# Where the last layer norm's VectorE work stands inside the next row pair's threshold search

## The chip, the cores and the metric

The kernel runs on one core of one Trainium2 chip. The metric is device time in microseconds (us); the kernel before takes 3777.57 us, the median of three runs (3777.3 to 3778.19). TensorE (PE) multiplies matrices, ScalarE (ACT) evaluates functions and copies, VectorE (DVE) and GpSimd (POOL) do elementwise work, and SyncE (SP) starts DMAs. Every engine works through its own queue in order and waits on semaphores for the others.

## The reference, cut to what matters

There are two graph layers on a matrix of N = 2708 rows and 512 columns. Each layer first takes `h = relu(layernorm(x))`, and its result is added to x. The first layer is a dense graph attention with 8 heads. The second, where the change is, makes two diffusion steps and ends with a layer norm of its own:

```python
for s in range(STEPS):                       # STEPS = 2
    A = _adj_from_feats(Xa, W1, W2, W3)      # nucleus attention, below
    Xf = Rf @ Xf
    Xb = Rb @ Xb
    Xa = A @ Xa
    Z = Z + (Xf @ U1[s] + Xb @ U2[s] + Xa @ U3[s])
Y = X + Z
mu = Y.mean(axis=-1, keepdims=True)
var = Y.var(axis=-1, keepdims=True)
return (Y - mu) / jnp.sqrt(var + LN_EPS) * gamma + beta

def _adj_from_feats(Xa, W1, W2, W3):
    logits = (Xa @ W1) @ W2 @ (Xa @ W3).T
    # per row: sort, cumulative softmax, keep the largest entries up to a mass of 0.9
    ...
    return jax.nn.softmax(masked, axis=1)
```

So in the last step every row needs logits against all 2708 keys, a threshold that keeps 90% of its softmax mass, the product of the kept weights with Xa, the three U products, and then the layer norm over its 512 columns, plus the residual x.

## The kernel before, in words

The rows lie in 22 tiles of 128 (the last has 20 rows). In the second layer they are worked in 11 pairs of tiles (`pairs`), and a loop `for g in range(-1, NP)` (L1158) runs over the pairs as a pipeline written out by hand: the orders on PE, ACT, DVE and SP are those of the program (`manual_schedule`, L1139). Only POOL's order is chosen by the planner of the framework, which goes by program order and by when it reckons an instruction ready.

One turn g of the loop, in the last step (s = 1), has in program order:

- `lg[g + 2].products()` (L509): the logits of pair g + 2. PE multiplies (L517), ACT copies from PSUM to the tiles p (L519, four of them).
- `normed` for the two tiles of pair g - 1, in the list `norms` (L1167). `normed` (L1074) takes the moments of the finished rows y at once: bn_stats and bn_aggr on DVE (L137, L138), then 1/sqrt on POOL (L139, L140). It starts the load of the residual xb on SP (L1079, tiles xw, two buffers shared with the load of L1067) and returns `rest`: two DVE instructions on 512 columns per tile (L1082, L1083) and the DMA of the result from POOL's queue (L1084).
- `search(lg[g + 1], ...)` (L593): DVE finds the threshold of pair g + 1. A head of small instructions brackets it from trial points; then `rounds` (L653) makes four rounds in this step (two in step 0). A round is a row of small instructions that choose a threshold th, one `mass` per tile (L624: all 2708 columns, two inputs, a sum) and small ones that narrow the bracket (L673 to L678). After the first round (`it == 0`) it calls `early()`, after `it == 1`'s threshold it calls what `early` returned.
- `early` (L1176) begins `exp()` of pair g + 2: the row maxima on DVE (L544); ACT's exponentials and their sums, POOL's trial points (`points`, L559 to L572, ending in the negated thresholds nth, L569) and ACT's twelve looks at them (L549) are put in the list `fills`. In the last step it returns a function that runs all `rest` of `norms`.
- `choose` (L692), then `late` (L1181): `attended` of pair g on PE. Its weights `keep` are transposed (L1004), copied by ACT (L1008, `at`) and multiplied with the values (L1023). `fills` and the diffusion products (`others`, L959) are dealt out between its steps. Then `mixed` (L1040) multiplies by U1, U2, U3 (L1051), and ACT (L1064) and POOL (L1068) put together the rows y that the next turn norms.
- `finish` (L793): DVE writes `keep` of pair g + 1 (L800, first of all; two buffers, which are those that PE has read for pair g) and extracts the cut; a switch on a value (L884) runs further instructions where entries are tied (L736 to L752). `rden` (L901) is its last instruction.

In the last turn (g = 10) there is no search: `normed` and `rest` of pair 9 run directly (L1203). After the loop those of pair 10 follow.

Of the kernel before, what the change touches and what calls it, by code (L numbers as in the profile page):

```python
# [53 lines left out]
def kernel(  # L54
# [77 lines left out]
    def moments(pool, src, pr):  # L132

        st = pool.tile([P, 6], F32, name="ln_st")
        mv = pool.tile([P, 2], F32, name="ln_mv")
        rs = pool.tile([P, 1], F32, name="ln_rs")
        nc.vector.bn_stats(st[:pr], src)  # L137
        nc.vector.bn_aggr(mv[:pr], st[:pr])  # L138
        nc.gpsimd.tensor_scalar(rs[:pr], mv[:pr, 1:2], LN_EPS, None, op0=OP.add)  # L139
        nc.gpsimd.tensor_tensor(rs[:pr], rs[:pr], nhalf[:pr], OP.pow)  # L140
        return mv[:pr, 0:1], rs[:pr]
# [346 lines left out]
    class Logits:  # L488
# [33 lines left out]
        def exp(self, looks=True):  # L522
# [68 lines left out]
            return steps  # L591

    def search(lg, looked, early, late):  # L593

        (wide, small, _), grp, ps_, tot, thr, s = lg.pools, lg.grp, lg.p, lg.tot, lg.thr, lg.s
        v = nc.vector
        nx = NEXT[s]
# [18 lines left out]
        def aim(dst, th):  # L618
            v.scalar_tensor_tensor(dst, th, AIM[s], lg.cap, op0=OP.mult, op1=OP.min)
            v.scalar_tensor_tensor(dst, tot, 1.0 - P_NUC + CURVE, dst, op0=OP.mult, op1=OP.add)  # L620
            v.reciprocal(dst, dst)

        def mass(i, pr, th, dst):
            v.scalar_tensor_tensor(junk_b[:pr], ps_[i][:pr], th, ps_[i][:pr],  # L624
                                   op0=OP.is_ge, op1=OP.mult, accum_out=dst)
# [27 lines left out]
        def rounds(n, aim_at=None):  # L653
            for it in range(n):
                v.tensor_tensor(d, ends[:, 1, 0:2], ends[:, 0, 0:2], op=OP.subtract)
                v.tensor_scalar(d[:, 1], d[:, 1], -1e-12, None, op0=OP.min)
                v.reciprocal(fr, d[:, 1])
                v.tensor_mul(fr, fr, ends[:, 0, 1])
                v.tensor_scalar(fr, fr, -0.95, -0.05, op0=OP.max, op1=OP.min)
                v.tensor_mul(fr, fr, d[:, 0])  # L660
                v.tensor_tensor(cur[:, 0], ends[:, 0, 0], fr, op=OP.subtract)
                v.tensor_mul(th, cur[:, 0], cur[:, 0])
                v.tensor_mul(th, th, th)
                if it in (aim_at or ()):
                    v.tensor_copy(fr, g0)
                    aim(g0, th)
                    v.tensor_tensor(fr, fr, g0, op=OP.subtract)
                    v.tensor_tensor(ends[:, :, 1], ends[:, :, 1], fr.unsqueeze(1).to_broadcast([P, 2, G]), op=OP.add)
                if it == 1 and begun:
                    begun.pop()()  # L670
                for i, pr in tiles:
                    mass(i, pr, th[:pr, i:i + 1], cur[:pr, 2, i:i + 1])
                v.tensor_tensor(fr, lg.top, cur[:, 2], op=OP.subtract)  # L673
                v.reciprocal(fr, fr)
                v.tensor_tensor(cur[:, 1], fr, g0, op=OP.subtract)
                v.scalar_tensor_tensor(side, cur[:, 1].unsqueeze(1).to_broadcast([P, 2, G]), 0.0, sides,
                                       op0=OP.is_ge, op1=OP.not_equal)
                v.copy_predicated(ends, side.unsqueeze(2).to_broadcast([P, 2, 3, G]),  # L678
                                  cur.unsqueeze(1).to_broadcast([P, 2, 3, G]))
                if it == 0 and aim_at is not None:  # L680
                    begun.append(early())

        begun = []
        rounds(ROUNDS[s], (0,) if s else ())
# [219 lines left out]
    for s in range(STEPS):  # L904
        last = s == STEPS - 1
        with ExitStack() as st:
# [20 lines left out]
            def values():  # L927
                for t in range(NT):
                    nc.sync.dma_start(out=va[:rows[t], t, :], in_=(xa_d if last else va_d)[cols[t], :])
# [49 lines left out]
            def paced(steps, n):  # L979
                for step in steps[:n]:  # L980
                    step()
                del steps[:n]

            def diffused(grp):
                out_ = []
                for i in range(2):
                    for t in grp:
                        x = work.tile([P, D], F32, name=f"x{i}")
                        nc.sync.dma_start(out=x[:rows[t]], in_=xfb_d[i, cols[t], :])
                        out_.append(x)  # L990
                return out_[:len(grp)], out_[len(grp):]
# [82 lines left out]
            def normed(t, y):  # L1074

                pr = rows[t]
                mean, rs = moments(small, y[:pr], pr)
                xb = work.tile([P, D], F32, name="xw", bufs=2)
                nc.sync.dma_start(out=xb[:pr], in_=xb_d[cols[t], :])  # L1079

                def rest():
                    nc.vector.scalar_tensor_tensor(y[:pr], y[:pr], mean, g_b[:pr], op0=OP.subtract, op1=OP.mult)  # L1082
                    nc.vector.scalar_tensor_tensor(y[:pr], y[:pr], rs, xb[:pr], op0=OP.mult, op1=OP.add)  # L1083
                    nc.gpsimd.dma_start(out=out[cols[t], :], in_=y[:pr])  # L1084

                return rest
# [52 lines left out]
            with tc.manual_schedule(engines={PE, ACT, DVE, SP}):  # L1139
                counted, spread = ranks() if last else (None, None)  # L1140
                lg = [Logits(pools, s, grp, keys, rank) for grp in pairs[:1]]
                lg[0].queries()
                lg[0].products()
                steps = lg[0].exp(looks=False)
                if last:
                    counted()
                for step in steps:
                    step()
                half = []
                lg += [Logits(pools, s, grp, keys, rank) for grp in pairs[1:2]]  # L1150
                lg[1].queries()
                for step in part(half, 0):
                    step()
                values()
                done = []
                ready = None
                looks, left = [], []
                for g in range(-1, NP):  # L1158

                    fills = []  # L1160
                    if g + 2 < NP:
                        lg[g + 2].products()
                    paced(looks, len(looks))
                    if g + 3 < NP:
                        lg.append(Logits(pools, s, pairs[g + 3], keys, rank))
                        lg[g + 3].queries()
                    norms = [normed(t, y) for t, y in done] if last else []  # L1167
                    done = []

                    rows_in = []  # L1170
                    if g >= 0:
                        left.append(lambda g=g: rows_in.extend(diffused(pairs[g])))
                    others = left + part(half, g + 2)
                    left = []

                    def early(g=g):  # L1176
                        if g + 2 < NP:
                            fills.extend(lg[g + 2].exp())
                        return lambda: [rest() for rest in norms]

                    def late(g=g):  # L1181
                        if g >= 0:
                            keep, rden = ready
                            if g:
                                paced(others, 1)
                            xa, v_t = attended(pairs[g], keep, rden, fills, others, lambda: turned_rows(pairs[g], rows_in[0]))
                            done.extend(mixed(pairs[g], v_t, rows_in[1], xa, others, fills))
                            paced(others, len(others))
                            paced(fills, len(fills))
                            return  # L1190


                        if last:
                            spread()
                        paced(fills, 5 + G * NA)
                        paced(others, NT if last else NT - NT // 2)
                        looks.extend(fills)
                        left.extend(others)

                    if g + 1 < NP:  # L1200
                        ready = search(lg[g + 1], g >= 0, early, late)
                    else:
                        for rest in norms:  # L1203
                            rest()
                        late()
                if last:
                    for rest in [normed(t, y) for t, y in done]:
                        rest()
# [31 lines left out]
```

## Time and profile before

| | |
|---|---|
| median of 3 runs | 3777.57 us |
| the profiled execution | 3774.21 us, of which the span from first to last instruction 3772.1 us |
| PE, busy share of the span | 90% |
| DVE | 69% |
| ACT | 41% |
| POOL | 22% |
| DMA | 167 GB/s of HBM traffic over the span |
| mean granted TensorE clock | 0.956 |

The last step runs from about 2430 us to the end of the span. The page shows shares of the whole span, so a single stage has to be read from the timeline: each line there has the start in us from the span's start, the duration in us, engine, line of the kernel, operation, output<-inputs, shapes, and how many equal instructions were merged. In square brackets stand the idle time of the engine just ahead of it and the instruction that ended this idle time. In lists of waits the three numbers are the total in us, how many times, and the longest in us.

### The profile page before, as it was taken

The page shows a single profiled execution, that of the slowest core. Times are in us where ns is not written, and L with a number is a line of the kernel's source. Part 1 is how long each engine was busy: PE and PEld are TensorE (multiplying, and loading weights), DVE is VectorE, ACT ScalarE, POOL GpSimd, SP SyncE. Part 2 cuts the span into 40 slices and gives each one's busy share as a digit, 9 for nine tenths or more (in the row PEclk, how much of TensorE's full clock was granted, in tenths as well). Part 3 has the DMA queues.
Part 4 walks back from the last instruction along what each step waited for, and adds up shares of the span by engine and source line. Part 5 has one row for each costly group of instructions (what it writes and reads, how often), then busy time and mean ns, then how long its engine had stood idle before and what let it go on. Part 6 is the DMA issues. An engine that isn't in the chain of part 4 may idle for free. (4 is left out here: it accounts for less than half of the span.)

```text
span 3772.1 us, 35425 instructions
## 1 busy us (share of the span) xinstructions
PE 3383.3 (90%) x11143; PEld 1760.6 (47%) x11143; DVE 2611.1 (69%) x4814; ACT 1540.1 (41%) x2334; POOL 838.2 (22%) x1187
## 2 busy tenths in 40 slices
PE   8999999999855898989898998668999999999988
PEld 4433333333533455545454453435555665556443
DVE  4588888989946526474554641967779798777992
ACT  2343202111025565546566621335544556445511
POOL 4115151423331121121212020302121211212101
PEclk9999999999977999999999998989999999999989
DMA  3476424233154554454545352845556665567552
GB/s 115 159 255 219 155 78 140 85 99 114 44 167 143 193 197 158 154 184 146 195 146 206 114 176 83 302 130 206 187 202 225 229 209 192 197 212 243 184 192 88
DMA packets 276457, 634.07 MB, mean 168 GB/s; under 512 B 37209, under 2 KB 70441, under 8 KB 273243
## 3 DMA queue, kind: packets, MB, share of 16 engines
q1 hardware_dynamic: 249183, 540.99, 43.3%
q0 software_dynamic: 27024, 90.30, 6.3%
q8 instruction: 89, 1.46, 0.2%
q14 instruction: 161, 1.32, 0.1%
HBM read 509.07 MB, written 122.10 MB: 167 GB/s over the span
## 5 line engine op out<-in xcount | busy, mean ns | idle before, releaser
L1023 PE MATMUL a<-va,at 128*128 128x512 f32 (+2 forms) x1936 | 898.0, 603 | 58.0 <-ACT at L1008 57.9
L959 PE MATMUL q<-hl,s_r 128*128 128x512 f32 x2904 | 821.8, 429 | 67.2 <-DMA s_r<-s_d 65.7
L429 PE MATMUL po<-e,fw 128*65 128x512 f32 (+4 forms) x2112 | 840.4, 553 | 30.0 <-DVE e L427 22.2
L427 DVE SCALAR_TENSOR_TENSOR e<-r_b,kk,a_c 128x512 f32<-128x512 f32 (+4 forms) x1056 | 752.3, 741 | 68.8 <-PE po L429 18.2
L959 PEld LDWEIGHTS q<-hl,s_r 128*128 128x128 f32 x2904 | 545.8, 190 | 312.4 <-issue 147.5
L549 ACT ACTIVATE junk_a<-p,nth 128x2708 uint8<-128x2708 f32 (+1 forms) x240 | 613.0, 2554 | 93.2 <-POOL nth L569 89.6
L429 PEld LDWEIGHTS po<-e,fw 128*65 128x65 f32 (+1 forms) x2112 | 286.5, 140 | 544.2 <-issue 269.1
L1023 PEld LDWEIGHTS a<-va,at 128*128 128x128 f32 (+2 forms) x1936 | 339.6, 188 | 428.2 <-issue 347.2
L1051 PE MATMUL a<-u_k,v_t 128*128 128x512 f32 (+1 forms) x1056 | 490.8, 601 | 20.9 <-ACT xa L1031 15.1
L624 DVE SCALAR_TENSOR_TENSOR junk<-p,th 128x2708 bf16<-128x2708 f32 (+1 forms) x132 | 402.2, 3047 | 4.0
L1008 ACT COPY at<-t 128x512 f32<-128x512 f32 (+3 forms) x308 | 139.8, 476 | 439.4 <-PE t L1004 439.2
L1051 PEld LDWEIGHTS a<-u_k,v_t 128*128 128x128 f32 (+1 forms) x1056 | 188.6, 186 | 239.6 <-issue 187.0
L517 PE MATMUL t<-keys,q_t 128*128 128x452 f32 x528 | 167.9, 444 | 117.0 <-ACT p L519 95.0
L800 DVE SCALAR_TENSOR_TENSOR keep<-p,th 128x2708 f32<-128x2708 f32 (+1 forms) x44 | 133.4, 3033 | 132.4 <-PE t L1004 131.1
L181 DVE TENSOR_SCALAR split_hl<-xe 128x512 int32<-128x512 int32 (+1 forms) x44 | 19.0, 432 | 275.6 <-ACT xe L965 232.6
L802 DVE MAX8 vn<-keep 128x8 f32<-128x2708 f32 (+1 forms) x66 | 196.8, 2981 | 2.3
L519 ACT COPY p<-t 128x452 f32<-128x452 f32 (+2 forms) x264 | 132.7, 539 | 149.8 <-DVEq L884 78.9
L517 PEld LDWEIGHTS t<-keys,q_t 128*128 128x128 f32 x528 | 91.8, 211 | 188.7 <-ACT p L519 149.5
L411 ACT ACTIVATE s_c<-a_c 128x512 fp32r<-128x512 f32 (+3 forms) x132 | 76.2, 577 | 248.3 <-DMA a_c<-in_adj_t_dram 123.2
L1004 PE MATMUL t<-ident,keep 128*128 128x128 f32 (+1 forms) x968 | 146.4, 273 | 21.9 <-DVE keep L752 16.5
L1004 PEld LDWEIGHTS t<-ident,keep 128*128 128x128 f32 (+1 forms) x968 | 114.5, 138 | 105.1 <-issue 76.9
L544 DVE TENSOR_REDUCE nmx<-p 128x1 f32<-128x2708 f32 (+1 forms) x44 | 129.2, 2966 | 40.3 <-ACT p L519 40.1
(294 smaller groups left out, 3105.1 us busy)
## 6 DMA issues: line engine op xcount, KB each, us to landing
s_r<-s_d SPq DMA_DIRECT2D x330, 256.0 KB
hl<-vhl_d SPq DMA_DIRECT2D x132, 512.0 KB
u_k<-in_L_gnn_U_dram SPq DMA_DIRECT2D x264, 256.0 KB
hl<-fhl_d SPq DMA_DIRECT2D x132, 512.0 KB
hl<-bhl_d SPq DMA_DIRECT2D x132, 512.0 KB
arow<-in_adj_dram SPq DMA_DIRECT2D x21, 1354.0 KB
s_d<-s_c SPq DMA_DIRECT2D x88, 256.0 KB
a_c<-in_adj_t_dram SPq DMA_DIRECT2D x84, 256.0 KB
```

The lines of the kernel that those rows point to most:

```text
L427: nc.vector.scalar_tensor_tensor(e[:pr, :cw], r_b[:pr, i, :cw], kk[:pr, t, hd:hd + 1], a_c[t][:pr, :cw], op0=OP.max, op1=OP.mult)
L429: nc.tensor.matmul(po[i][:, :cw], lhsT=fw[:pr, t, hd, :], rhs=e[:pr, :cw], start=(t == 0), stop=(t == NT - 1))
L517: nc.tensor.matmul(pl[:, :c1 - c0], lhsT=q[:, i], rhs=self.keys[:, c0:c1], start=(i == 0), stop=(i == 1))
L549: nc.scalar.activation(junk[:pr], self.p[i][:pr], func, **kw)
L624: v.scalar_tensor_tensor(junk_b[:pr], ps_[i][:pr], th, ps_[i][:pr], op0=OP.is_ge, op1=OP.mult, accum_out=dst)
L800: v.scalar_tensor_tensor(keep[i][:pr], ps_[i][:pr], t, ps_[i][:pr], op0=OP.is_lt, op1=OP.mult, accum_out=left[:pr, i:i + 1] if e else None)
L802: v.max(vs, keep[i][:pr])
L959: nc.tensor.matmul(half[j], lhsT=s_r[:, j * P:(j + 1) * P], rhs=hl[:, h], start=(c == 0 and h == 0), stop=(c == NT - 1 and h == 1))
L1004: nc.tensor.transpose(pt[:rows[c], j, :pr], keep[i][:pr, cols[c]], ident[:pr, :pr])
L1008: nc.scalar.copy(at[:r, j0:j1, :pr], pt[:r, j0:j1, :pr])
L1023: nc.tensor.matmul(pa[:pr], lhsT=at[:rows[c], j, :pr], rhs=va[:rows[c], c, :], start=(c == 0), stop=(c == NT - 1))
L1051: nc.tensor.matmul(pz[i][:rows[t]], lhsT=v_t[i][:, k, :rows[t]], rhs=u_k, start=(n == 0 and k == 0), stop=(n == 2 and k == KD - 1))
```

## The change

`early` returns a list of two functions instead of one function, and `rounds` runs one of them per round, ahead of the masses, from `it == 2` on. The first calls `normed` for both tiles (the moments, the load of xb), the second runs their `rest`. So at the head of the turn nothing of the layer norm is left; its moments stand ahead of the masses of the third round, and its end ahead of those of the fourth, where before they stood ahead of the search and ahead of the masses of the second. `norms` now holds the pairs (t, y) themselves; the last turn makes `normed` of them directly. In step 0 `norms` is empty, as before.

```diff
@@ rounds, in search @@
-                if it == 1 and begun:
-                    begun.pop()()
+                if it > 1 and begun:
+                    begun.pop(0)()
                 for i, pr in tiles:
                     mass(i, pr, th[:pr, i:i + 1], cur[:pr, 2, i:i + 1])
...
                 if it == 0 and aim_at is not None:
-                    begun.append(early())
+                    begun.extend(early())
@@ the loop over the pairs @@
-                    norms = [normed(t, y) for t, y in done] if last else []
+                    norms = done if last else []
                     done = []
...
                     def early(g=g):
                         if g + 2 < NP:
                             fills.extend(lg[g + 2].exp())
-                        return lambda: [rest() for rest in norms]
+                        held = []
+                        return [lambda: held.extend(normed(*x) for x in norms), lambda: [rest() for rest in held]]
...
                     else:
-                        for rest in norms:
+                        for rest in [normed(*x) for x in norms]:
                             rest()
                         late()
```

## The prediction

> **What bounds the kernel now.** I read the page first. TensorE is busy 90% of the span, VectorE 69%; so VectorE time counts only where TensorE stands waiting for it.
>
> ```profile
> span 3772.1 us, 35425 instructions
> PE 3383.3 (90%) x11143; PEld 1760.6 (47%) x11143; DVE 2611.1 (69%) x4814; ACT 1540.1 (41%) x2334; POOL 838.2 (22%) x1187
> ```
>
> Then the waits of the second step (2500 to 3772 us). VectorE loses 159.2 us to the statistics that the change moves, 63.1 of them in one wait at the end of the kernel, which stays. TensorE waits for VectorE once, 16.5 us.
>
> ```profile
> DVE ln_st L137 <- POOL yo L1068: 159.2, 18, 63.1
> PE t L1004 <- DVE keep L752: 16.5, 1, 16.5
> ```
>
> Third, TensorE's timeline. I call "turn g" the stretch that starts with the normed rows of pair g-1, holds the search of pair g+1 on VectorE, and attended and mixed of pair g on TensorE. Turns 1 to 8 follow each other every 116.7 us (their first statistics start at 2660.3, 2776.3, ... 3360.5, 3477.1) with TensorE nearly full (114.0 of 116.6 us in turn 7). Only turn 9 begins late: the search in turn 8 meets a tie and ends at 3597.9, while TensorE was done at 3581.5.
>
> ```profile
> 3526.71 3.70 PE L1023 MATMUL a<-va,at 128*128 128x512 f32 x8 [1.55 <-ACT at L1008]
> 3532.10 0.38 PE L1004 MATMUL t<-ident,keep 128*128 128x128 f32 x2
> 3598.07 1.94 PE L1004 MATMUL t<-ident,keep 128*128 128x128 f32 x8 [16.53 <-DVE keep L752]
> ```
>
> Fourth, VectorE in turn 8: done with pair 8 at 3464.8, it waits 12.30 us for the mixed rows; then the search's head and first round, the maxima of pair 10 (L544), the other rounds, and the first write of each keep tile (L800, 3528.67 and 3541.21).
>
> ```profile
> 3464.66 0.17 DVE L901 RECIPROCAL rden<-den 128x2 f32<-128x2 f32 x1 [7.09 <-issue]
> 3477.13 0.69 DVE L137 BATCH_NORM_STATS2 ln_st<-yo 128x6 f32<-128x512 f32 x1 [12.30 <-POOL yo L1068]
> 3492.28 5.83 DVE L544 TENSOR_REDUCE nmx<-p 128x1 f32<-128x2708 f32 x2
> 3511.64 3.04 DVE L624 SCALAR_TENSOR_TENSOR junk<-p,th 128x2708 bf16<-128x2708 f32 x1
> 3514.72 3.04 DVE L624 SCALAR_TENSOR_TENSOR junk<-p,th 128x2708 bf16<-128x2708 f32 x1
> 3541.21 3.02 DVE L800 SCALAR_TENSOR_TENSOR keep<-p,th 128x2708 f32<-128x2708 f32 x1
> ```
>
> Last, the two engines that feed each other beside it, ScalarE and GpSimd, in turn 8. The logits of pair 10 are copied by 3485.11. GpSimd's trial points (L561 to L572) wait for ScalarE's sums, and ScalarE's looks (L549) wait 6.53 us for their result nth; behind two looks stands the copy that TensorE waited 1.55 us for.
>
> ```profile
> 3484.16 0.95 ACT L519 COPY p<-t 20x452 f32<-20x452 f32 x2 [0.34 <-PE t L517]
> 3520.86 2.55 ACT L549 ACTIVATE junk_a<-p,nth 128x2708 uint8<-128x2708 f32 x1 [6.53 <-POOL nth L569]
> 3526.09 0.57 ACT L1008 COPY at<-t 128x512 f32<-128x512 f32 x1
> ```
>
> ```profile
> 3508.96 0.72 POOL L562 TENSOR_TENSOR x<-half,powers 128x2 f32<-128x2 f32 x1 [5.33 <-ACT junk_a L549]
> 3512.54 2.69 POOL L561 TENSOR_TENSOR x<-tot,powers 128x2 f32<-128x2 f32 x1 [2.86 <-ACT p L556]
> 3515.22 2.64 POOL L570 TENSOR_SCALAR thr<-tot 128x2 f32<-128x2 f32 x1
> 3520.58 0.25 POOL L569 TENSOR_SCALAR nth<-th_a 128x6 f32<-128x6 f32 x1
> ```
>
> **What the Trainium skill says.** "SBUF — State Buffer", section "Who interferes with whom": a VectorE instruction with two SBUF inputs contends with a GpSimd instruction that reads SBUF; a tensor_reduce never does. The trace agrees. L561, started inside a mass (L624, two inputs), took 2.69 us; in a gap between masses (2560.14) it took 0.69. L570 took 2.64 in a mass, 0.23 in a gap (2439.79). Every held one ends 0.1 to 0.6 us after the mass. MAX8 (one input) holds none: L566 beside it takes 0.22. "GPSIMD Engine Reference", section "Key points", says the same of the shared interfaces. So where VectorE's masses lie decides when GpSimd's points end.
>
> **The change, part by part.** It applies to turns 1 to 9; step one has no normed rows, its lists are empty.
>
> Removed: the wait at the head (12.3 us in most turns, 17.5 in turn 1, 0.8 in turn 3, 0 in turn 9). What is late next: L544 of the second logits tile, which cannot start before 3485.11 + about 0.05. VectorE would be ready for the first at 3464.8 + 13.1 (from the 15.15 us between 3477.13 and 3492.28, less 2.06 of statistics) = 3477.9, but its tile is copied at 3481.25; so the first reduction ends near 3484.2 and the second near 3488.1, instead of 3498.1: 10.0 us earlier.
>
> Moved: four statistics instructions per turn now stand before the third mass pair: 1.54 us without waits (turn 9 shows them so, 3598.04 to about 3599.6). Left on the way to keep: 10.0 - 1.5 = 8.5 us. The four rest instructions take 3.0 us (3499.69 to 3502.70) wherever they stand: nothing. The y rows were ready at 3477, some 20 us before they are asked for. The xb loads on SyncE keep their place, since the rounds issue nothing there. L139/L140 on GpSimd get 9 us until L1083 needs rs. The two out DMAs go 10 us later (L1083 at about 3510.6 and 3512.1 instead of 3501.3 and 3502.8), past the points on GpSimd's queue; their own cost is 0.55 to 0.63 each. The xw and yo buffers are wanted again about 100 us later.
>
> Turns 1 to 7: TensorE sets the pace, so the earlier search gains nothing. There the next wait is the second keep tile: TensorE reads it until 60.8 us into the turn (3421.3 in turn 7), VectorE wrote it at 64.1 and would now write at 55.6, so 3 of the 8.5 us remain, and they end as slack.
>
> Turn 8: TensorE's last read of keep is 3532.48, the wanted write 3541.21 - 8.5 = 3532.7: it just fits, if TensorE isn't later. It will be. In the new order the fourth masses run 34.85 to 37.9 and 37.9 to 41.0 us into the turn (the old third ones 34.5 to 40.6), but after them comes choose and L800 2.0 us later, where another round left 2.8 us (3517.76 to 3520.58). GpSimd's chain needs 3.0 us in that gap, and used all of it. Now the last three or four of its instructions fall into L800 (42.9 to 46.0) and end at about 46.7 instead of 43.7: nth 3.1 us later. In turn 8 nth goes straight on to the copy at 3526.09, to TensorE's L1023 and its last read of keep: 3532.5 + 3.1 = 3535.6. So keep comes 5.5 us earlier, not 8.5, and TensorE starts turn 9 that much earlier. The rest follows unchanged (VectorE works through turn 9, TensorE through turn 10): -5.5.
>
> Turns 1, 2, 4 to 7 have slack for 3.1 us: the copy ends at 49.5 and is asked for at 53.35; the xa copy behind the looks moves by 3.1 less 2.36 of ScalarE's idle time there, 0.7, with 0.9 to spare. Cost 0 to 0.1.
>
> Turn 3 starts late behind the tie of turn 2 (VectorE done 2894.7, now about 2891.6), so its masses lie 6.5 us later than in the other turns; statistics held by masses on GpSimd push L562 to 36.4, then rest and two masses hold the chain: nth near 48.5, 4.8 late. The copy ends at 54.3 against 53.35 and xa 0.5 later still: TensorE loses about 1.6 us.
>
> Sum: -5.5 + 1.6 = -3.9 us. The profiled execution took 3774.21 (span 3772.1, 2.1 around it), 3.4 under the median of 3777.57: 3774.2 - 3.9 = 3770.3 there, 3773.7 at the median.
>
> **What is unknown.** GpSimd's order is the planner's, not written out: L1084 stood before L562, and could again. Bounds of that are the rivals below; I take L562 first because its input comes at 31.8 us and the first out row only at 33.7.
>
> **The rivals.**
> 1. Full gain: nth isn't later in turn 8 and nothing is lost elsewhere. For it: a hold hangs on tenths of a microsecond. Against: L561 and L570 land in masses in every turn. -8.5: 3769.1.
> 2. Outs between L562 and L561. Only turn 3 changes: the second out issues at 42, L561 and L570 are held by the two masses to 47.6, one more falls into L800: nth near 53.5, TensorE 6.4 late. -5.5 + 6.4 = +0.9: 3778.5.
> 3. Slower: both outs ahead of L562. L562 then starts at 35.7 in a mass, L561 in the next, L800 catches one more: nth 3.9 to 4.3 late in every turn. From 3.9 on, the copy and xa come too late for TensorE: at 4.3 it loses 0.5 + 0.55 in each of six turns (6.3), 7.3 in turn 3, and turn 8 gains 4.3. +9.3: 3786.9. It decides from about 4.1; at 3.9 it is +6. For it: L1084 comes first in the program. Against: it is ready later.
>
> **How the numbers follow.** About 0.2% (7.6 us) is what can be told from no change. Forecast 0.34 (own range 3770 to 3778), full gain 0.29, rival 2 0.12, rival 3 0.25. Rival 1 lies over the bound, forecast and rival 2 within it; of rival 3 a fifth stays within, of the forecast a little lies beyond on the fast side: faster 0.30, same 0.47, slower 0.23. Range: from the full gain with half a microsecond of spread, 3768.5, to rival 3 less its tail, 3787.
>
> **What would show it.** Right: L137 without a wait, in its place one at L544 for ScalarE's p copy; in turns 1 to 7 a wait of L800 for TensorE's t L1004; nth 46 to 47 us into the turn; TensorE's wait before turn 9 about 8 us and its 1.55 grown to 4.6; turns still 116.7 us apart, turn 3 longer. Wrong: turns 1 to 7 longer by 0.5 us or more each (rival 3), TensorE's 1.55 unchanged (rival 1), or L1083 waiting for rs because L139 was put behind the points.

## The result, and the profile after

The changed kernel takes 3789.05 us (median of 13 runs, 3784.33 to 3792.64), against 3778.2 us of the kernel before beside it (median of 13, 3777.0 to 3782.27). The ratio is 1.0027, with a 95% interval of 1.002 to 1.0034: slower by 7.6 to 12.8 us. The forecast was 3.9 us faster.

The profiled execution took 3789.2 us, just the median; that of before took 3774.21, 4.0 under its median of these runs. So the 15.0 us between the two spans, which are accounted for below, are some 4 more than the distance of the two medians, 10.85.

The page of the changed kernel, first its head and the busy time of the engines:

```profile
span 3787.1 us, 35425 instructions
PE 3382.7 (89%) x11143; PEld 1759.6 (46%) x11143; DVE 2612.6 (69%) x4814; ACT 1538.4 (41%) x2334; POOL 896.5 (24%) x1187
```

The same instructions, the same busy time on TensorE and VectorE; GpSimd is busy 58 us longer, in instructions that are held. So nothing was added to the work: TensorE stands still for longer. Where, the waits of the second step say (2500 to 3787 us; total, times, longest):

```profile
ACT junk_a L549 <- POOL nth L569: 73.4, 8, 16.7
...
DVE keep L801 <- PE t L1005: 55.6, 9, 13.4
DVE nmx L544 <- ACT p L519: 54.0, 14, 10.3
...
PE a L1024 <- ACT at L1009: 30.3, 11, 15.7
...
PE t L1005 <- DVE keep L753: 8.8, 1, 8.8
PE t L1005 <- DVEq L885: 8.4, 1, 8.4
```

(Lines from 595 on are one higher than before.) The head's wait L137 is gone except for the last of the kernel, and its time went to L544 and L801. ScalarE's wait for nth, at most 6.5 us before, has one of 16.7. TensorE still waits for keep once, 8.8 instead of 16.5 us, but its waits in L1024 and for L885, the switch of the tied entries, have grown, from 19.4 to 30.3 and from 1.5 to 8.4 us. (The 15.7 us in L1024 stand ahead of turn 1 and were there before.) TensorE's timeline shows the three that matter (start, duration, and in brackets the idle time ahead):

```profile
2955.45 6.42 PE L1024 MATMUL a<-va,at 128*128 128x512 f32 x8 [8.02 <-ACT at L1009]
...
3541.71 5.13 PE L1024 MATMUL a<-va,at 128*128 128x512 f32 x8 [4.63 <-ACT at L1009]
...
3703.17 1.94 PE L1005 MATMUL t<-ident,keep 128*128 128x128 f32 x8 [8.44 <-DVEq L885]
3704.93 5.44 PE L1024 MATMUL a<-va,at 128*128 128x512 f32 x8
```

The first is new and stands in turn 3; the second was 1.55 in turn 8; the third stands ahead of turn 10 and was 1.50, as TensorE's timeline of the kernel before has it:

```profile
3690.45 1.06 PE L1004 MATMUL t<-ident,keep 128*128 128x128 f32 x8 [1.50 <-DVEq L884]
3691.75 3.70 PE L1023 MATMUL a<-va,at 128*128 128x512 f32 x8 [0.24 <-ACT at L1008]
```

Cut at TensorE's own work, the second step comes out as follows, in us, for these two kernels and for those of the experiments. Turns 1 to 8 run from the first logits product (L517) to the next turn's; turn 8 ends, and turn 9 and the tail (turn 10 and the end) begin, with the first transposes of keep behind the idle time.

| kernel | turn 3 | turn 8 | turn 9 | tail | span |
|---|---|---|---|---|---|
| before | 116.65 | 122.66 | 92.38 | 81.64 | 3772.1 |
| after | 128.50 | 118.19 | 97.66 | 83.91 | 3787.1 |
| outs on SyncE's queue | 122.25 | 119.08 | 97.37 | 87.30 | 3784.0 |
| only the end moved | 116.67 | 121.71 | 93.57 | 83.28 | 3777.5 |
| only in turn 8 | 116.67 | 120.62 | 97.12 | 82.86 | 3777.2 |
| one round sooner | 122.29 | 119.47 | 96.81 | 83.89 | 3786.1 |
| before, no ties | 116.65 | 106.96 | 96.13 | 84.23 | 3762.5 |
| after, no ties | 116.67 | 109.14 | 92.06 | 82.45 | 3757.7 |
| only in turn 8, shifted | 116.67 | 120.79 | 102.06 | 83.48 | 3780.6 |
| put off | 116.67 | 114.42 | 89.04 | 81.96 | 3764.4 |
| 64 memsets at the start | 127.35 | 120.48 | 97.90 | 84.03 | 3785.6 |
| y added later | 127.16 | 118.51 | 96.52 | 83.06 | 3783.9 |

All other turns last 116.1 to 116.7, and one, sometimes two, per run 117.5 to 117.6: there some matmuls of the logits take 0.75 instead of 0.47 us, in any kernel and in changing turns. From before to after: turn 3 +11.85, turn 8 -4.47, turn 9 +5.28, tail +2.27, the rest +0.1: +15.0.

Each row is one execution, and the row of before is a short one. Taken from the start of turn 1 to the end, each of the eleven other kernels comes out 1.9 to 5.5 us slower against before in these traces than its median does against the median of before beside it. Turns 1 to 7 are alike in all rows but for turn 3. So the row of before probably lacks about 4 us in turn 8, turn 9 and the tail, and what other rows lose against it there is too large by about as much in sum.

### The profile page after: what moved, and what is told of

The parts are those of the page before. It is cut to its first block, busy times and chain, and to the rows that moved or that the text cites. A ratio compares the mean times of both kernels' runs of the same rounds, so it can differ in the third digit from the quotient of the medians.

```text
span 3787.1 us, 35425 instructions
## 1 busy us (share of the span) xinstructions
PE 3382.7 (89%) x11143; PEld 1759.6 (46%) x11143; DVE 2612.6 (69%) x4814; ACT 1538.4 (41%) x2334; POOL 896.5 (24%) x1187
## 5 line engine op out<-in xcount | busy, mean ns | idle before, releaser
L1024 PE MATMUL a<-va,at 128*128 128x512 f32 (+2 forms) x1936 | 901.9, 605 | 70.6 <-ACT at L1009 70.6
L1024 PEld LDWEIGHTS a<-va,at 128*128 128x128 f32 (+2 forms) x1936 | 341.3, 189 | 443.2 <-issue 349.7
L517 PE MATMUL t<-keys,q_t 128*128 128x452 f32 x528 | 170.1, 450 | 114.5 <-ACT p L519 91.6
L801 DVE SCALAR_TENSOR_TENSOR keep<-p,th 128x2708 f32<-128x2708 f32 (+1 forms) x44 | 133.7, 3039 | 176.5 <-PE t L1005 175.3
L544 DVE TENSOR_REDUCE nmx<-p 128x1 f32<-128x2708 f32 (+1 forms) x44 | 129.9, 2969 | 91.1 <-ACT p L519 91.1
L517 PEld LDWEIGHTS t<-keys,q_t 128*128 128x128 f32 x528 | 92.9, 213 | 187.3 <-ACT p L519 146.5
```

Source lines behind the costliest of these rows:

```text
L517: nc.tensor.matmul(pl[:, :c1 - c0], lhsT=q[:, i], rhs=self.keys[:, c0:c1], start=(i == 0), stop=(i == 1))
L801: v.scalar_tensor_tensor(keep[i][:pr], ps_[i][:pr], t, ps_[i][:pr], op0=OP.is_lt, op1=OP.mult, accum_out=left[:pr, i:i + 1] if e else None)
L1024: nc.tensor.matmul(pa[:pr], lhsT=at[:rows[c], j, :pr], rhs=va[:rows[c], c, :], start=(c == 0), stop=(c == NT - 1))
```

## The experiments

Two accounts stood open after the two traces. One (A, in the expectations) says that the loss comes with the ties: turn 3, behind the tie of turn 2, loses through a late nth, and turn 9 and the tail, behind the tie of turn 8, through a VectorE that is late. The rivals, named in each expectation, say that it comes from elsewhere: from the order of the queues in every turn, or from the moved work itself. Times are medians of the runs; the kernel before, run beside each set, had 3779.9 (48 runs), 3777.05 (27) and 3777.66 us (27).

**The out DMAs away from GpSimd.** GpSimd in turn 3 of the changed kernel:

```profile
2932.43 0.69 POOL L562 TENSOR_TENSOR x<-half,powers 128x2 f32<-128x2 f32 x1
2936.62 0.63 POOL L1085 DMA_DIRECT2D out_dram<-yo  x1 [3.50 <-DVE yo L1084]
2938.13 0.55 POOL L1085 DMA_DIRECT2D out_dram<-yo  x1 [0.88 <-DVE yo L1084]
2938.69 2.67 POOL L561 TENSOR_TENSOR x<-tot,powers 128x2 f32<-128x2 f32 x1
2941.35 2.61 POOL L570 TENSOR_SCALAR thr<-tot 128x2 f32<-128x2 f32 x1
...
2946.19 2.77 POOL L567 TENSOR_TENSOR th_a<-pts 128x6 f32<-128x6 f32 x1
...
2949.32 0.24 POOL L569 TENSOR_SCALAR nth<-th_a 128x6 f32<-128x6 f32 x1
```

The outs stand between L562 and L561, as in rival 2 of the prediction. GpSimd waits for the rows of VectorE's `rest`, 3.50 and 0.88 us, with its next point ready behind them; and when it gets to L561, VectorE's fourth masses (2937.75 to 2943.8) hold it. This kernel issues the outs from SyncE instead, behind attended, and the last ones behind the loop.

```diff
-                    nc.gpsimd.dma_start(out=out[cols[t], :], in_=y[:pr])
+                    sent.append(lambda: nc.sync.dma_start(out=out[cols[t], :], in_=y[:pr]))
...
+                            paced(sent, len(sent))
...
+                    paced(sent, len(sent))
```

> As the changed kernel, but the DMA of the normed rows (L1085 there) is issued from SyncE's queue behind the attended stage, so that nothing on GpSimd's queue stands between L562 and L561. Theory A (in turn 3, which starts late behind a tie, GpSimd's points wait behind the two output DMAs, and TensorE behind the points): nth of turn 3 comes some 4.7 us earlier than in the changed kernel (about 51.5 instead of 56.5 us into the turn), TensorE's stall there falls from 8.0 to about 3.3 us, turn 3 takes 121 to 123 us instead of 128.5, and the whole is 6 to 8 us faster than the changed kernel, 3 to 5 slower than before. Rival B (the late masses of VectorE hold the points by themselves, the DMAs are innocent): turn 3 stays above 126 us. The other turns stay at 116.65 in both.

Measured: 3790.3 us (11 runs), ratio 1.0029 (1.002 to 1.0038). In the place itself it went as A has it. GpSimd of turn 3:

```profile
2932.03 0.69 POOL L562 TENSOR_TENSOR x<-half,powers 128x2 f32<-128x2 f32 x1
2932.69 0.70 POOL L561 TENSOR_TENSOR x<-tot,powers 128x2 f32<-128x2 f32 x1
2933.38 0.25 POOL L570 TENSOR_SCALAR thr<-tot 128x2 f32<-128x2 f32 x1
...
2940.56 3.04 POOL L569 TENSOR_SCALAR nth<-th_a 128x6 f32<-128x6 f32 x1
```

nth is 5.2 us sooner in the turn, TensorE's wait falls from 8.02 to 3.65 us, turn 3 from 128.5 to 122.25. So the outs' place costs turn 3 some 5.4 us (0.87 of the 6.25 are slower logits, see above). But the whole isn't faster in the timed runs than the changed kernel (1.0029 against 1.0027): the expected 6 to 8 us were not found. In its profile the tail gives 3.4 us back, and these lie behind TensorE's last product (TensorE's own part of the tail takes 73.0 us here and 73.1 in the changed kernel). The last out, too, is issued from SyncE, and the span ends 8.27 us after VectorE's last instruction, where it ends 4.1 to 4.9 us after it in all eleven other kernels, which issue it from GpSimd. First the end of the changed kernel (span 3787.1), then that of this one (3784.0):

```profile
3781.60 0.74 DVE L1084 SCALAR_TENSOR_TENSOR yo<-yo,ln_rs,xw 20x512 f32<-20x512 f32 x1
3782.63 0.54 POOL L1085 DMA_DIRECT2D out_dram<-yo  x1 [0.76 <-DVE yo L1084]
```

```profile
3774.31 1.79 SPq L1085 DMA_DIRECT2D out_dram<-yo  x2
3775.02 0.74 DVE L1084 SCALAR_TENSOR_TENSOR yo<-yo,ln_rs,xw 20x512 f32<-20x512 f32 x1
```

So this kernel repairs turn 3 and pays for it at the end: of the 5.4 us some 1.9 should be left, less than these runs can tell from nothing.

**Only the end moved.** The statistics stay at the head; `rest` runs ahead of the fourth round.

```diff
-                    norms = done if last else []
+                    norms = [normed(t, y) for t, y in done] if last else []
...
-                        return [lambda: held.extend(normed(*x) for x in norms), lambda: [rest() for rest in held]]
+                        return [lambda: None, lambda: [rest() for rest in norms]]
...
-                        for rest in [normed(*x) for x in norms]:
+                        for rest in norms:
```

> Half of the change: the end of the layer norm (rest) ahead of the fourth round, the statistics at the head of the turn as before. Theory A (the loss comes of the early start of the search, which shifts the masses against GpSimd's points, once the statistics no longer hold it): all turns as before, turn 3 at 116.7 us, TensorE's wait for keep ahead of turn 9 at 16.5 us, the whole within 2 us of before. Rival C (the late rest with its output DMAs is what costs): turn 3 longer by 5 us or more, or every turn longer by 1 us or more.

Measured: 3777.76 us (13 runs), ratio 0.9997 (0.9988 to 1.0005): no change from before. Turn 3 is 116.67; the planner put the outs behind nth here. So the end's later place, by itself, costs nothing, with that order of the queue; the outs between L562 and L561, with the statistics at the head, were not run. The loss appears only together with the moved statistics, which pull the search forward.

**The change in turn 8 alone.** The other turns as before.

```diff
-                if it > 1 and begun:
+                if it > 0 and begun:
...
-                    norms = done if last else []
+                    norms = [] if not last else done if g in (NP - 3, NP - 1) else [normed(t, y) for t, y in done]
...
+                        if g != NP - 3:
+                            return [lambda: [rest() for rest in norms]]
...
+                        return [lambda: None, lambda: held.extend(normed(*x) for x in norms), lambda: [rest() for rest in held]]
```

> The change in turn 8 alone; in turns 1 to 7 the statistics stand at the head and rest ahead of the second round as before. Theory A: turn 3 is 116.7 us again (11.8 less than in the changed kernel); turn 8 keeps its gain of about 4.5 us at the start of turn 9; what turn 9 and the tail give back (5.3 and 2.3 us in the changed kernel's profile) comes back if it is of turn 8's making: then the whole is 0 to 4 us slower than before; if it was an accident of that execution: 3 to 5 us faster than before. Rival B' (the change costs in every turn): between before and the changed kernel by an eighth.

Measured: 3778.33 us (13 runs), ratio 0.9998 (0.999 to 1.0006). Turn 3 is back at 116.67, turn 8 gains 2.0, turn 9 loses 4.7 and the tail 1.2. So in the trace the loss behind the tie of turn 8 is made by turn 8 alone, with turn 9 left as it was; turn 3's is a separate one. In the timed runs the change in turn 8 alone is no change (between 3.8 us faster and 2.3 slower): what it gains is about used up behind the tie. So the 10.85 us that the whole change loses in the timed runs go with the other turns, of which only turn 3 became longer by more than 1 us.

**Everything one round sooner.** Statistics ahead of the second round, the end ahead of the third.

```diff
-                if it > 1 and begun:
+                if it > 0 and begun:
```

> The whole change one round sooner: statistics ahead of the second round, rest ahead of the third, so that the output DMAs stand ahead of L562 on GpSimd's queue and are issued 9 us earlier. Theory A: nth of turn 3 at about 51 us instead of 56.5, turn 3 at 120 to 123 us instead of 128.5, turns 1, 2, 4 to 7 at 116.7, turn 8 as in the changed kernel: 6 to 8 us faster than the changed kernel. Rival B (masses alone): turn 3 above 126 us.

Measured: 3785.25 us (22 runs), ratio 1.0013 (1.0007 to 1.002). Turn 3 takes 122.29 us, the same as with the outs on SyncE; turn 8, turn 9 and the tail are those of the change within 1.3 us. The round matters for turn 3, not for what follows the tie of turn 8. Here the last outs stay on GpSimd, and a shorter turn 3 shows in the timed runs too: by the ratios (1.0013 against 1.0027, intervals that just touch) this kernel is some 5 us faster than the changed one.

**No ties.** In the last step the switch's arm of tied entries is left empty, in the kernel before and in the changed one.

```diff
                 if 0 < arm < 1 << G:
-                    ties([x for x in tiles if arm >> x[0] & 1])
+                    if not (lg.rank is not None):
+                        ties([x for x in tiles if arm >> x[0] & 1])
```

> The kernel before with the further work on tied entries left out in the last step (the switch's arms for ties are empty; the rows with ties keep all tied entries). For comparison with the next run. TensorE's wait ahead of turn 9 goes; VectorE then waits for the normed rows in turn 9 and ends some 92 us later: 12 to 16 us faster than before.

> The changed kernel with the same work on ties left out. Theory A (the loss lies only in the turns that a tie makes late: turn 3 behind the tie of turn 2, turn 9 behind that of turn 8): no turn of 1 to 7 above 117.6 us; against the run without ties of the kernel before 4 us faster to 1 us slower. Rival B' (the shifted masses cost something in every turn): 8 us slower or more than that run.

Measured: 3764.04 us (5 runs), ratio 0.9966 (0.9953 to 0.9979), for the kernel before, and 3761.82 (6 runs), 0.9963 (0.995 to 0.9976), for the changed one. Without ties the change isn't slower. No turn of 1 to 7 loses anything, though nth is 3 us later in each, as in the changed kernel; so rivals that put the loss into every turn fall, and A holds: turn 3's and the later loss come with the ties.

**Why turn 9 loses: a shifted turn 8.** The kernel with the change in turn 8 alone, and 40 more small memsets on VectorE at the head of turn 8.

```diff
+                    if g == NP - 3 and last:
+                        pad = small.tile([P, G], F32, name="pad", bufs=1)
+                        for _ in range(40):
+                            nc.vector.memset(pad, 0.0)
```

> As the run with the change in turn 8 alone, with 40 VectorE memsets of one small tile more at the head of turn 8, where VectorE waits for the copied logits anyway; they only move where the following instructions lie. In all runs with the change in turn 8, VectorE's first instruction behind the tie (the reciprocal rden) came 2.6 to 3.1 us late, without it 0.04 us. Theory D (instruction fetch: it depends on where the code behind the switch lies): the gap falls under 0.5 us, VectorE ends the search of turn 9 ahead of GpSimd's y additions, and the whole is 3 to 5 us faster than with the change in turn 8 alone. Rival E (it is the time at which the tie ends): the gap stays 2.6 to 3.1 us, and so does the whole within 1 us.

Measured: 3783.04 us (22 runs), ratio 1.0017 (1.0011 to 1.0024). It was not 3 to 5 us faster; turn 9 became longer (102.06), partly because the switch's next use let TensorE go 6.4 us behind VectorE's last instruction ahead of it, where it takes 1.45 us before. A miss: it moves too much at once to tell anything, save that the gap described next stayed (2.91 us).

**Why turn 9 loses: where instructions stand, or the y additions.** VectorE behind the tie of turn 8 in the changed kernel, and GpSimd beside it:

```profile
3597.26 1.04 DVE L749 SCALAR_TENSOR_TENSOR fr<-p,over 128x1 f32<-128x1 f32 x1
3598.34 4.00 DVE L751 SCALAR_TENSOR_TENSOR junk<-p,fr,junk 128x2708 bf16<-128x2708 f32 x1
3602.38 2.98 DVE L753 SCALAR_TENSOR_TENSOR keep<-junk,keep 128x2708 f32<-128x2708 bf16 x1
...
3608.45 0.17 DVE L902 RECIPROCAL rden<-den 128x2 f32<-128x2 f32 x1 [3.09 <-issue]
```

```profile
3596.53 2.97 POOL L1069 TENSOR_TENSOR yo<-yo,xw 128x512 f32<-128x512 f32 x2 [1.52 <-ACT yo L1065]
```

The same in the kernel before, where the additions (L1068, from 3581.39, 2.86 us) meet other instructions of the arm:

```profile
3581.95 1.09 DVE L742 TENSOR_TENSOR over<-den,thr 128x2 f32<-128x2 f32 x1
...
3583.15 1.11 DVE L744 TENSOR_TENSOR over<-over,fr 128x2 f32<-128x2 f32 x1
...
3591.86 3.04 DVE L750 SCALAR_TENSOR_TENSOR junk<-p,fr,junk 128x2708 bf16<-128x2708 f32 x1
...
3597.96 0.17 DVE L901 RECIPROCAL rden<-den 128x2 f32<-128x2 f32 x1
```

Two things are to be seen. In both kernels the additions hold VectorE twice in the arm, for about 1.9 us together; that is even. But after the change there is an idle gap of 3.09 us ahead of rden, with no one to wait for ("issue"). The trace's records of the queue that fetches instructions show an 8 KB fetch 1.8 to 1.9 us ahead of rden in both (that it is VectorE's is inferred from its time): before it starts during the arm's last pass, after the change only 1.2 us behind its end. Two theories: the place of the instructions in the stream (64 memsets instead of one at the kernel's start, where VectorE waits for data, shift all of it), or the held pass L751 (GpSimd's additions of pair 8 are put off behind 45 memsets).

```diff
-    nc.vector.memset(sides[:, 0], 0.0)
+    for _ in range(64):
+        nc.vector.memset(sides[:, 0], 0.0)
```

```diff
+                    if last and grp == pairs[-3]:
+                        if i == 0:
+                            pad = small.tile([P, 32], F32, name="pad", bufs=1)
+                            nc.gpsimd.tensor_copy(pad, y[:, :32])
+                            for _ in range(45):
+                                nc.gpsimd.memset(pad, 0.0)
+                        nc.gpsimd.tensor_tensor(y[:pr, :32], y[:pr, :32], pad[:pr], op=OP.add)
                     nc.gpsimd.tensor_tensor(y[:pr], y[:pr], z[:pr], op=OP.add)
```

> The changed kernel with 64 more memsets on VectorE at the very start of the kernel, where VectorE waits for its first data (1.0 to 7.9 us): they cost nothing themselves, and move all later VectorE instructions by 64 places in its stream. The question is why rden (L902) starts 3.09 us after the last instruction of the tie's arm of turn 8 (no gap in the kernel before). Theory L (where instructions stand in the stream, and so when the stretch behind the arm is fetched): the gap changes, to under 0.3 us if it goes, and turn 9 falls from 97.7 to between 92.5 and 95 us, the span from 3787.1 to 3782 to 3784. Theory H (the y additions of GpSimd, which hold the last but one pass of the arm for 0.96 us, shift the fetch): nothing changes, gap 2.6 to 3.1, turn 9 97 to 98, span within 2 us of 3787.

> The changed kernel with the y additions of pair 8 (L1069) about 6 us later on GpSimd, behind 45 small memsets (and an addition of the zeros to 32 columns of y, which changes no value): they then start near 3602.5 instead of 3596.5 and no longer hold the arm's L749 and L751 (1.04 and 4.00 us, unheld 0.16 and 3.04), but at most its last pass L753. Theory H (the hold on L751 makes the gap): gap under 0.3 us, keep written about 1 us sooner, turn 8 117 to 118 us, turn 9 92.5 to 95, span 3780 to 3784. Theory L: keep is sooner by 1 to 2 us all the same, but the gap stays at 2.6 to 3.1 us and turn 9 at 96.5 to 98.5.

Measured, memsets at the start: 3790.55 us (8 runs), ratio 1.0034 (1.0022 to 1.0045). L751 is held again (4.00 us), the gap is 3.72 us, turn 9 takes 97.9. Measured, y added later: 3784.98 us (20 runs), ratio 1.0022 (1.0015 to 1.0029), and on VectorE:

```profile
3597.92 0.16 DVE L749 SCALAR_TENSOR_TENSOR fr<-p,over 128x1 f32<-128x1 f32 x1
3598.11 3.04 DVE L751 SCALAR_TENSOR_TENSOR junk<-p,fr,junk 128x2708 bf16<-128x2708 f32 x1
...
3604.21 0.17 DVE L902 RECIPROCAL rden<-den 128x2 f32<-128x2 f32 x1
...
3606.29 1.57 DVE L649 COPY_PREDICATED ends<-below,pts 128x6 f32<-128x6 int32 x3
```

With L751 free the gap is gone (0.04 us), as theory H has it. Over all ten kernels whose tie runs, the six with L751 at 4.00 us have a gap of 2.6 to 3.7 us, and the four with 3.04 (before, only the end moved, put off, y added later) have none. In the arm of turn 2, where L751 takes 3.04 us in all ten, it is at most 0.35 us. Nor is it just any hold: in the version put off the additions hold the arm's last pass (3.92 instead of 2.98 us), and there is no gap. The place in the stream, moved by 63 instructions, did not remove it. Yet turn 9 fell only to 96.52, not to the expected 92.5 to 95: the additions now run beside the head of turn 9 (the last line: 1.57 us where 0.58 is usual, and so a second time), and the first mass starts 8.0 instead of 6.1 us behind rden: 97.66 - 3.05 + 1.9 = 96.5. Those of pair 9 still hold small instructions at the search's end, for 2.0 us. Turn 8 did not shorten either, since its tie began 2.2 us later in the turn. A hold that is moved out of the way came back at the next place.

**A version that does without the stages around the tie.** In the kernel before, the layer norms of pairs 7 and 8, due in turns 8 and 9, are put off to turn 10, where VectorE has no search; their y rows wait in HBM.

```diff
-                    if not last:
+                    if not last or grp in pairs[-4:-2]:
                         nc.gpsimd.dma_start(out=y_d[cols[t], :], in_=y[:pr])
...
+                    if last and NP - 3 <= g < NP - 1:
+                        done = []
...
+                        for grp in pairs[-4:-2] if last else []:
+                            for rest in [normed(*again(t), nc.gpsimd) for t in grp]:
+                                rest()
```

> The kernel before, with the layer norm of pairs 7 and 8 taken out of turns 8 and 9 altogether: their rows y go to DRAM and are normed in turn 10, where VectorE waits 63 us. Turn 8 has neither statistics nor rest nor the wait for them. If what limits the gain is what VectorE has to do in turns 8 and 9: keep ahead of turn 9 comes 8 to 10 us earlier than before, turn 9 loses its 4.5 us of VectorE work and TensorE's second wait shrinks to 0 to 3 us; the whole is 8 to 13 us faster than before. If the late first instruction behind the tie and the y additions hit here too, 3 to 7 us faster.

Measured: 3764.8 us (6 runs), ratio 0.9967 (0.9956 to 0.9979): faster than before by 7.9 to 16.6 us, and better than either kernel. Turn 8 takes 114.42 instead of 122.66 us, turn 9 89.04 instead of 92.38. That is what the change was after, the wait and the statistics out of VectorE's way in the turn where TensorE stands waiting for it, without pushing VectorE's masses into GpSimd's points.

## Why the prediction failed, step by step

**Right: what replaces the head's wait.** L137 waits no more; L544 waits for ScalarE's p (54.0 us in all), L801 for TensorE (55.6 us in nine). Turns 1, 2 and 4 to 7 neither gain nor lose (116.15 to 117.55 against 116.09 to 117.5), though nth comes 2.9 to 4.1 us later in each.

**Right: nth in turn 8.** 3.1 us later, as worked out; TensorE's 1.55 became 4.63, as named. This rests on "SBUF — State Buffer", section "Who interferes with whom", in the Trainium skill: a VectorE instruction with two SBUF inputs contends with a GpSimd one that reads SBUF. The trace agrees (L561 2.67 beside a mass, 0.70 without, in the two kernels of turn 3 above).

**Smaller by a fifth: turn 8's gain.** 5.5 us were predicted, 4.47 came. The second keep tile was written 4.2 us sooner within the turn. Missing is that TensorE works slower after the stall: its next eight products took 5.13 instead of 3.70 us, and L801 waits for the last reader.

**Wrong: "Turn 3 starts late ... TensorE loses about 1.6 us".** It lost 11.85. Four terms:
- nth in the predicted order. The kernel with the outs on SyncE has that order, and nth ends at 51.3 us into the turn (counted as in the prediction), not at 48.5. L562 starts at 39.7 instead of 36.4: L139 and L140 of the second tile, 2.81 and 3.35 us long, were held by the two masses of the third round. That is the whole of it: from L562 to nth it took 11.6 us, against 12.1 worked out. TensorE stalls 3.65 us, not 1.6.
- The order itself: "I take L562 first" was right, but the outs come second, as in rival 2. That is another 4.4 us of stall (8.02 less 3.65). Rival 2 had 6.4 for both.
- The slow start afterwards, in no term of mine or of any rival: 6.42 instead of 3.60 us for eight products, 2.8 us (1.8 with the shorter stall).
- 0.87 us of slower logits, which do not belong to the change.

**Wrong: "The rest follows unchanged (VectorE works through turn 9, TensorE through turn 10)".** Turn 9 lost 5.28 and the tail 2.27. Of the 5.28, 3.09 are the gap ahead of rden. 2.0 are GpSimd's additions of pair 9, which used to run when VectorE was through the small instructions of `finish`; VectorE is now later against them, and they hold it, as VectorE's and GpSimd's timelines of the changed kernel show:

```profile
3695.59 1.16 DVE L827 TENSOR_TENSOR fr<-sn,thr 128x2 f32<-128x2 f32 x1
3696.78 1.19 DVE L828 TENSOR_TENSOR fr<-fr,thr 128x2 f32<-128x2 f32 x1
```

```profile
3694.58 3.37 POOL L1069 TENSOR_TENSOR yo<-yo,xw 128x512 f32<-128x512 f32 x2 [1.62 <-ACT yo L1065]
```

(0.11 and 0.16 us when free.) The remaining 0.2 lie between the head and the search's end. In before the additions just miss VectorE; how often they do, its one profile cannot tell. The tail's 2.27 are TensorE's start after 8.44 instead of 1.50 us of idle time: 7.04 instead of 4.84 us from the first transposes to the next ones.

So from -3.9 to +15.0 there are 18.9 us: turn 3 has 10.25 of them (4.0 in the predicted order, 5.4 through the order, 0.87 slower logits), turn 8's smaller gain 1.0, and turn 9 with the tail, which had no term, 7.55. The timed runs are 10.85 us slower, not 15.0, and the 4 us between are probably the short execution of before. So by the timed runs the gain of turn 8 is about used up behind its tie (the change in turn 8 alone is no change), and turn 3, with 11.85 instead of 1.6, is about the whole loss. Rival 3, slower by 9.3 us through both outs ahead of L562 in every turn, is near the measured total for a reason that did not occur: the outs stood elsewhere, and six turns of the seven lost nothing.

What stays open: why a held L751 delays the fetch of the instructions behind the arm. That the two go together is shown, by ten traces and by the kernel that frees L751; how is not. The jump out of the arm is not what is late: it stands 0.11 us behind the start of the last pass in all 20 arms of the ten traces. The fetch follows it by 1.0 to 1.5 us in 14 of them, and by 3.7 to 4.7 us in the six whose L751 was held. How the 4 us that the execution of before lacks are shared among turn 8, turn 9 and the tail, one profile of it cannot tell.

## What to carry to other kernels

A stage that falls out of step, here the turn behind a tie, has to be worked through by itself: a moved block that fits everywhere else meets other masses there, and a queue whose order a planner sets decides how much. To a stall of the engine that sets the pace belongs its slow start afterwards; count it for every stall that a change makes, and for every one it removes. And where work is moved within an engine that others wait for, moving it out of the stage that is late altogether (here to the last turn, 0.33% faster) can beat the places inside it (here all that were tried). Last, a single profile can be a short one: set its distance from the others against the timed runs before a loss is booked to a stage.

## What the runs showed of the hardware

TensorE after idle time. An fp32 product 128x128 by 128x512 takes 0.59 us in flow, and one starts every 0.43 us; the first ones behind a stall take 1.22 and 1.06, and one starts every 0.85. After 1.50 us idle only 3.70 us were needed for eight; after 2.74 us (the kernel with only the end moved), 5.31; after 4.63, 5.13; after 8.02, 6.42. The Trainium skill, "TensorE: Matmul & The Clock Gate", section "Part 1: The HAM clock gate (the "warmup" mystery)", says that the array falls to half its clock after an idle window of about 3.4 us and comes back after about 3.4 us of work, with a window that runs freely. The halved rate agrees, and so does a loss of 1.4 to 2.8 us that varies; but here 2.74 us of idle time were already enough, while 3.46 us (y added later) were not (the two products behind them took 1.12 us, against 1.02 in flow):

```profile
3694.24 1.06 PE L1005 MATMUL t<-ident,keep 128*128 128x128 f32 x8 [2.74 <-DVEq L885]
3695.54 5.31 PE L1024 MATMUL a<-va,at 128*128 128x512 f32 x8 [0.24 <-ACT at L1009]
```

```profile
3564.23 1.12 PE L1052 MATMUL a<-u_k,v_t 128*128 128x512 f32 x2 [3.46 <-ACT xa L1032]
```

In the first of these the slow products begin only 1.3 us after TensorE has started again.

GpSimd can hold VectorE's smallest instructions too. Two additions of 128x512 on GpSimd (2.5 to 3.4 us) stretch VectorE instructions of 0.11 to 0.17 us to 1.03 to 1.19, and one of 3.04 to 4.00, two per run of additions, about 2 us in all; moved, they held others for as long.

A switch's arm can end with a gap of its own: 2.6 to 3.7 us on VectorE with nothing to wait for, or 0.03 to 0.35, in kernels whose instructions there are the same.

Who issues the last DMA can decide the end: 4.1 to 4.9 us from VectorE's last instruction to the end of the span where GpSimd issues the last out, 8.27 us in the one kernel where SyncE does.
